# A two-layer Perceiver block on one core: normalization on VectorE, FP4 maxima in one reduce, biases added earlier, feed-forward split at 384 columns

## Chip, cores and metric

The kernel runs on one core of a Trainium2 chip. The metric is device time in microseconds. The kernel before took 1554.78 us, the median of three runs (1544.31 to 1555.05). Engines are named as in the profile: PE (matmul; PEld is its weight load), DVE (VectorE), ACT (ScalarE), POOL (GpSimd), SP (SyncE, which issues most transfers). An `Lnnn` is a line of the kernel before.

## What is computed

The input `x` has 16 sequences of 64 rows of 256 numbers, 1024 rows in all, and each sequence has a context of 1024 rows of 256. Each of two layers applies cross-attention to the context, self-attention and a feed-forward part, each on a layer-normalized copy of `x` and added back to it. In layer 0 self-attention goes across sequences, and the feed-forward part is a mixture of eight experts. The change concerns layer 1 (and the quantization of its weights). Cut to its core:

```
def _layernorm(x, eps=1e-05):
    m = mean(x); v = var(x)
    return (x - m) / sqrt(v + eps)

def fp4_quant_dequant(x):                 # blocks of 16 along the last dim
    scale = max(max(abs(xb)) / 6, 1e-12)
    xn = xb / scale
    idx = searchsorted(_MID, abs(xn))
    return _GRID[idx] * sign(xn) * scale

def _L1_xattn_ref(query, mem, ...):       # 16 heads of 16, bias and mask on keys
    return softmax(q @ k.T * scale + attn_bias + pad) @ v @ out_w.T + out_b

def _L1_attn_ref(x, w_qkv, w_proj, b_proj):   # rotary, 16 heads, 64 rows each
    return softmax(rope(q) @ rope(k).T * scale) @ v @ w_proj + b_proj

def _L1_ffn_ref(x, w_gate, w_up, w_down):     # 256 -> 704 -> 256
    h = silu(fp4(x) @ fp4(w_gate).T) * (fp4(x) @ fp4(w_up).T)
    return fp4(h) @ fp4(w_down).T

x = x + _L1_xattn_ref(_layernorm(x), ctx_1024, ...)
x = x + _L1_attn_ref(_layernorm(x), ...)
x = x + _L1_ffn_ref(_layernorm(x), ...)
```

## The kernel before

All data are 32-bit floats. The 1024 rows of `x` stay on chip as eight tiles `x[n]` of 128 rows (two sequences each). `consts` holds the identity for PE's transposes. PSUM has eight banks; in layer 1 seven rotate under the name `psw` (`bank()`), and one, `pso`, gathers attention outputs.

**Main loop of cross-attention.** Layer 1's cross-attention (`cross_attention`, L308 to L640) walks over 64 slots: 16 sequences x two groups of heads x two halves of the keys. Each slot issues on PE the scores of the slot after the next (L445), four groups of transposes of the exponentials `e` (L475), and the products of the slot before with `v` (L489). DVE reads the scores, adds the mask and finds the minimum (L456), ACT takes the exponential (L467), and both copy the transposes (L217, L219). Keys and values of nine sequences were made earlier and lie in DRAM; those of the other seven are projected inside the loop (L370, L385).

**Chains.** All work that follows on a pair of sequences is a Python generator, a *chain*, on row tile n. After every group of transposes the loop calls `advance()`, which runs each living chain on to its next `yield`, oldest first: four advances in a slot. A chain starts after the eighth slot of its pair, so a chain is 32 steps ahead of the next one while the loop lasts, and 28 at its end, where the last slot's work has no advances. PE's instructions are issued in exactly the order in which the program text produces them (`manual_schedule`); a PE instruction that waits holds up all behind it. The other engines' orders are made by a scheduler from dependences and its own estimates of duration. So the number of yields between two matmuls of a chain sets how much main-loop work lies between them on PE. When the loop is over, the two chains still living (n = 6 and n = 7) are advanced alternately until they end: the tail.

A chain's steps (the code between yields), counted from 1:

- `outputs`, steps 1 to 7: copy of `pso` (1), transposes L511 and division by the sums, L514 (3), transposes L527 and value bias, L531 (5), output projection `project_rows` L301 (7).
- `row_attention`: `layernorm_rows` (9), transposes L269 and copy L271 (12), queries and keys L1229, copy `ra` L1238, cosine part on POOL L1240 (14), rotation L1249 and sine part on DVE L1250 (16), sums L1258/L1259 and the masked queries `rqm` on POOL L1262 (17), values L1273 (18), scores L1286 and their minima and differences, L1297/L1298 (20, 21), exponential L1304 (22), transposes L1311 (24), products L1327 and sums L1338, reciprocal L1348 and L1349 (26, 27), projection L301 (29).
- `feed_forward`: `layernorm_rows` (31), FP4 of the 256 columns (34 to 37), transposes L269 (39), both halves of 352 hidden columns L1376, `Silu` L1379 and product L1380 (41), FP4 of the halves one after the other (42 to 49), all six transposes L1391 (51), down projection L1405, the last sum L1407 and the store L1408 (53).

**`layernorm_rows`** finds mean and variance on DVE (L244, L246), starts the reciprocal square root from the exponent bits (L248 to L253, DVE), makes three Newton steps of three instructions each on POOL, and applies the result on POOL (L260, 128x256). It then yields three times. It also serves the queries of cross-attention (`queries`, tile `xnq`, L269 and L405), which run ahead of the loop for n = 0 and in it for the others. `arrive` gathers the expert outputs of layer 0 for the next row tile by two indirect transfers on POOL (L1127) and adds them to `x[n]` on DVE (L1137) just before `xnq` is normalized.

**`fp4`** takes absolute values on ACT (L890), finds the blocks' maxima (L893), makes scale and reciprocal (L894 to L898), and scales (L899), rounds (L906 to L910) and scales back (L911) on DVE. `quantize_weights` uses it for the six weight blocks, beside layer 0's experts.

**`project_rows`** multiplies, adds the bias on DVE to `prow` (L303), and adds `prow` to `x[n]` on POOL (L304).

Of the kernel before, what the change touches and what calls it, by code (L numbers as in the profile page):

```python
# [19 lines left out]
P = 128  # L20
# [98 lines left out]
def kernel(ctx: ExitStack, tc: tile.TileContext, a: dict, out: bass.AP):  # L119
# [121 lines left out]
    def layernorm_rows(pool, n, name="xnr"):  # L241
# [55 lines left out]
    def project_rows(n, oT, w, bias):  # L297

        pm = bank()
        for c in range(KC):  # L300
            nc.tensor.matmul(pm[:, :D], oT[:, c, :], w[:, c, :], start=(c == 0), stop=(c == KC - 1))  # L301
        t = small.tile([P, D], F32, name="prow")
# [4 lines left out]
    def cross_attention(layer, wq, wkv, wo, bq, bk, bv, bo, mask, keep, bias, after, ready, arrive, idle):  # L307
        side = "right" if layer else "left"  # L308
        with ExitStack() as st:
# [84 lines left out]
            def queries(n):  # L394
# [3 lines left out]
                xn = yield from layernorm_rows(single, n, "xnq")  # L398
# [98 lines left out]
            def outputs(b):  # L497
# [38 lines left out]
                project_rows(n, oT, wo, rowbias(bo))  # L536
# [346 lines left out]
    def fp4(pool, dst, src, rows, n, tag, most=None):  # L883

        nb = n // BLK
        most = most or n
        shape = [rows, nb, BLK]
        t = pool.tile([P, most], F32, name=f"t{tag}")[:rows, :n]
        t3 = t.rearrange("p (g k) -> p g k", k=BLK)
        nc.scalar.activation(t, src, AF.Abs)  # L890
# [4 lines left out]
        rsc = pool.tile([P, most // BLK], F32, name=f"rsc{tag}")[:rows, :nb]  # L895
# [4 lines left out]
            t3, src.rearrange("p (g k) -> p g k", k=BLK), rsc.unsqueeze(2).to_broadcast(shape), ALU.mult  # L900
# [4 lines left out]
        m = pool.tile([P, most], F32, name=f"m{tag}")[:rows, :n]  # L905
# [257 lines left out]
    def quantize_weights(step, pool):  # L1163
        if step < 4:
# [9 lines left out]
            for _ in fp4(pool, q, raw, PG, n, "w"):  # L1174
# [12 lines left out]
        elif step < 6:  # L1187
# [4 lines left out]
            for _ in fp4(pool, q, raw, P, NI, "d"):  # L1192
# [15 lines left out]
    def last_layers(one):  # L1208
# [11 lines left out]
        def row_attention(n, two):  # L1220
            vz = vzs[n % 2]
            xn = yield from layernorm_rows(two, n)
# [134 lines left out]
            project_rows(n, oT, wproj, rowbias("L1_attn_b_proj"))  # L1357
# [3 lines left out]
        def feed_forward(n, two):  # L1361
            tok = slice(n * P, (n + 1) * P)
            xn = yield from layernorm_rows(two, n)
            yield from fp4(one, xn, xn, P, D, "h", NI)
# [5 lines left out]
            for g in range(2):  # L1370
                cols = slice(g * NH, (g + 1) * NH)
                pg = bank()[:, :NH]
                pu = bank()[:, :NH]
                for ps, w in ((pg, wgT), (pu, wuT)):
# [138 lines left out]
```

## Time and profile before

| | |
|---|---|
| median of three runs | 1554.78 us |
| profiled execution, its own time | 1553.52 us |
| its span, first to last instruction | 1551.8 us |
| mean granted PE clock | 0.942 |
| second layer's cross-attention begins (L269 on `xnq`) | at 871.6 us |
| last main-loop products (L489) end | at 1463.5 us |
| last store issued | at 1549.1 us |

Times within the run count from the first instruction. "Busy" is the time in which an engine works on an instruction. A row of the stage table gives a stretch, its length, and each engine's busy time in it (with the number of instructions), the granted PE clock as a share of full speed, the share of time that the transfers were busy, and GB/s. A row of the timeline gives start, duration, engine, line, operation, output from inputs, shapes, a count, and in brackets how long the engine was idle before it and what ended that. A row of the waits gives who waited for whom: time in total, number of times, the longest. The chain of waits that ended last:

```profile
PE 73%; DVE 12%; POOL 4%; ACT 4%; DMA 3%; issue 3%; ACTq 0%; POOLq 0%; DVEq 0%; SPq 0%
```

### The profile page before, as it was taken

To read this page: it belongs to the slowest core of one execution; us is meant where nothing else is said; L and a number is where in the kernel's file an instruction comes from. 1 tells how busy PE (TensorE), PEld (TensorE's weight loads), DVE (VectorE), ACT (ScalarE), POOL (GpSimd) and SP (SyncE) were. 2 spreads that over 40 slices of the span, in tenths; PEclk is the share of its full clock that TensorE was granted. 3 is DMA by queue.
4 is the path that set the end of the run, shared out by engine and by line. 5 is a ranking of instruction groups with operands and counts; after the bars stand their busy time and mean duration, and the time that the engine had idled before them with its cause. 6 is when DMAs were issued, how large, how long until landed. Compare 5 with 4: busy or idle time off the path is not lost.

```text
span 1551.8 us, 32601 instructions
## 1 busy us (share of the span) xinstructions
PE 1411.0 (91%) x13488; PEld 995.0 (64%) x13488; DVE 880.4 (57%) x2325; ACT 725.3 (47%) x1339; POOL 285.4 (18%) x502
## 2 busy tenths in 40 slices
PE   4999999999999998999999787888899999999754
PEld 2667766676667655768887555565657666666542
DVE  2556665656565533365721265675767675757543
ACT  2555555555555532223221475564656465646321
POOL 4101010000000031013300134241414141311111
PEclk8999999999999999999999798888889999999876
DMA  8111110101000021377774232322101111100000
GB/s 281 59 31 35 32 59 32 35 32 59 31 28 2 35 90 70 105 260 235 234 283 147 90 117 94 118 86 74 57 14 46 46 52 49 42 5 1 5 5 3
DMA packets 53073, 119.48 MB, mean 77 GB/s; under 512 B 4877, under 2 KB 24333, under 8 KB 50621
## 3 DMA queue, kind: packets, MB, share of 16 engines
q1 hardware_dynamic: 48876, 109.93, 21.0%
q0 software_dynamic: 1648, 4.72, 1.1%
q10 hardware_dynamic: 2400, 2.76, 0.5%
q8 instruction: 106, 1.74, 0.5%
q14 instruction: 43, 0.34, 0.1%
HBM read 94.32 MB, written 23.07 MB: 76 GB/s over the span
## 4 chain that ended last, share of the span: by engine, by line
PE 73%; DVE 12%; POOL 4%; ACT 4%; DMA 3%; issue 3%; ACTq 0%; POOLq 0%; DVEq 0%; SPq 0%
PE psw L475 11%; PE psw L385 10%; PE psw L370 9%; PE psw L445 8%; PE pso L489 7%; PE psw L659 4%; PE psw L1085 4%; PE psw L1105 4%; DVE e L456 3%; PE psw L646 3%; ACT e L467 3%; PE psw L1376 2%; PE psw L1405 2%; PE psw L301 2%; DMA kd<-astage 1%
## 5 line engine op out<-in xcount | busy, mean ns | idle before, releaser
L467 ACT ACTIVATE e<-e,mn 128x1024 f32<-128x1024 f32 x256 | 291.1, 1139 | 125.3 <-DVE mn L456 125.3
L475 PEld LDWEIGHTS psw<-consts,e 128*128 128x128 f32 x2048 | 242.6, 144 | 111.6 <-issue 64.3
L475 PE MATMUL psw<-consts,e 128*128 128x128 f32 x2048 | 286.8, 280 | 10.1 <-DVE mn L456 5.7
L456 DVE CUSTOM_DVE_ANT_0 e<-psw,negb,mn 128x512 f32<-128x512 f32 x256 | 177.9, 747 | 180.0 <-PE psw L445 180.0
L456 DVE CUSTOM_DVE_ANT_0 e<-psw,negb 128x512 f32<-128x512 f32 x256 | 162.9, 686 | 87.0 <-PE psw L445 86.8
L219 ACT COPY eT<-psw 128x512 f32<-128x512 f32 x320 | 174.1, 590 | 58.3 <-PE psw L475 57.9
L445 PE MATMUL psw<-kT,qm 32*128 32x512 f32 x1024 | 167.7, 690 | 3.4 <-ACT qm L415 1.8
L489 PE MATMUL pso<-eT,v 128*32 128x128 f32 x4096 | 146.0, 286 | 0.0
L370 PE MATMUL psw<-ctxT,w_L_xattn_Wkv 128*128 128x512 f32 x256 | 125.0, 612 | 11.9 <-DMA ctxT<-in_ctxT_dram 11.9
L217 DVE COPY eT<-psw 128x512 f32<-128x512 f32 x192 | 123.0, 678 | 9.3 <-PE psw L475 9.3
L489 PEld LDWEIGHTS pso<-eT,v 128*32 128x32 f32 x4096 | 109.4, 114 | 28.0 <-issue 25.9
L385 PE MATMUL psw<-w_L_xattn_Wkv,ctxT 128*128 128x256 f32 x512 | 123.6, 385 | 0.0
L385 PEld LDWEIGHTS psw<-w_L_xattn_Wkv,ctxT 128*128 128x128 f32 x512 | 93.0, 190 | 33.7 <-issue 11.9
L370 PEld LDWEIGHTS psw<-ctxT,w_L_xattn_Wkv 128*128 128x128 f32 x256 | 44.3, 192 | 68.4 <-issue 55.1
L219 ACT COPY v<-psw 128x512 f32<-128x512 f32 x46 | 27.0, 588 | 123.8 <-PE psw L385 123.8
L304 POOL TENSOR_TENSOR x<-x,prow 128x256 f32<-128x256 f32 x24 | 17.4, 727 | 315.1 <-DVE prow L303 315.1
L659 PE MATMUL psw<-w_L_xattn_Wkv_w,actx 128*128 128x256 f32 x288 | 73.4, 409 | 0.8 <-ACT astage L653 0.8
L445 PEld LDWEIGHTS psw<-kT,qm 32*128 32x128 f32 x1024 | 49.2, 197 | 37.8 <-issue 20.2
L337 POOL TENSOR_SCALAR negb<-m 128x1024 f32<-128x1024 uint8 x16 | 16.7, 1046 | 285.8 <-DVE mn L456 172.4
L380 ACT ACTIVATE kT<-psw,colb 128x512 f32<-128x512 f32 x48 | 32.8, 687 | 75.3 <-PE psw L370 75.3
L646 PE MATMUL psw<-actx,w_L_xattn_Wkv_w 128*128 128x512 f32 x144 | 66.2, 599 | 1.3 <-DVE x L632 1.3
L659 PEld LDWEIGHTS psw<-w_L_xattn_Wkv_w,actx 128*128 128x128 f32 x288 | 58.0, 206 | 13.6 <-issue 3.8
(248 smaller groups left out, 1974.0 us busy)
## 6 DMA issues: line engine op xcount, KB each, us to landing
ctxT<-in_ctxT_dram SPq DMA_DIRECT2D x23, 1024.0 KB, 5.0
w<-in_L_ffn_w_dram SPq DMA_DIRECT2D x16, 1024.0 KB, 6.9
actx<-in_ctxT_dram SPq DMA_DIRECT2D x9, 1024.0 KB, 6.8
kd<-astage SPq DMA_DIRECT2D x36, 256.0 KB, 3.7
vd<-astage SPq DMA_DIRECT2D x36, 256.0 KB, 2.4
kT<-kd SPq DMA_DIRECT2D x9, 1024.0 KB, 6.1
v<-vd SPq DMA_DIRECT2D x9, 1024.0 KB, 5.0
ab<-in_fside_BxS_dram SPq DMA_DIRECT2D x32, 256.0 KB, 3.4
```

The costliest lines, as they stand in the source:

```text
L217: nc.vector.tensor_copy(dst, src)
L219: nc.scalar.copy(dst, src)
L370: nc.tensor.matmul(pm, wkv[:, c, dt * P : (dt + 1) * P], ctxT[b][:, c, cols], start=(c == 0), stop=(c == KC - 1),)
L385: nc.tensor.matmul(pm[:, j * D : (j + 1) * D], ctxT[b][:, c, (k + j) * P : (k + j + 1) * P], wkv[:, c, D : 2 * D], start=(c == 0), stop=(c ...
L445: nc.tensor.matmul(sc[g], qm[b // 2][r : r + 32, dt, b % 2, :, :].rearrange("p j q -> p (j q)"), kT[b][r : r + 32, dt, cols], start=True, ...
L456: nc.vector.tensor_tensor_reduce(out=e[:, cols], in0=sc[g], in1=negb[b][:, cols], scale=1.0, scalar=3e38 if hf == 0 else mn[b][:, 0, pr : ...
L467: nc.scalar.activation(e, e, AF.Exp, scale=-1.0, bias=mn[b][:, 1, pr : pr + 1], accum_out=sums[b][:, pr : pr + 1])
L475: nc.tensor.transpose(pt[:, g * P : (g + 1) * P], es[b, dt, g][:, k * P : (k + 1) * P], ident)
L489: nc.tensor.matmul(po[b][32 * g : 32 * g + 32, dt, :], v[b][:, k, pr * 32 : (pr + 1) * 32], e[:, g, :], start=(k == 0), stop=(k == NK - 1),)
L646: nc.tensor.matmul(pm, w1kv[:, c, dt * P : (dt + 1) * P], actx[b][:, c, cols], start=(c == 0), stop=(c == KC - 1),)
L659: nc.tensor.matmul(pm[:, j * D : (j + 1) * D], actx[b][:, c, (k + j) * P : (k + j + 1) * P], w1kv[:, c, D : 2 * D], start=(c == 0), stop=( ...
L1085: nc.tensor.matmul(ph[:, j * CAP : (j + 1) * CAP], w1[:, c, (f + j) * P : (f + j + 1) * P], xeT[:, c, :], start=(c == 0), stop=(c == KC - 1),)
```

## The change

`layernorm_rows` gets a switch `vector`. With it, all Newton steps run on DVE, two instructions each (the factor -0.5 is multiplied into the variance once), the result is applied on DVE, and the function doesn't yield. It is set for `row_attention`, `feed_forward` and layer 1's first query tile; the other query tiles and layer 0 keep POOL. `row_attention` yields twice of its own instead of three times, `feed_forward` once.

In layer 1 `project_rows` no longer adds a bias: the product is added to `x[n]` by one DVE instruction. The biases are added to `x[n]` on POOL as soon as the normalized copy has been made: the output bias after `xnq`, the projection bias after `xnr`.

`fp4` has no ACT step and no yield for it: the reduce takes absolute values itself. Its tiles are made by a function of their own, so that two calls can work on parts of the same tiles.

The hidden columns are split 384 and 320 (three PE transposes each). For n up to 6 each half has its own step for matmuls and for transposes. For n = 7 (`alone`) everything from the first hidden matmul on is one step, in which the first half's transposes and its share of the down projection come ahead of the second half's quantization.

The chain's steps after the change, counted in the same way: `outputs` as before; `row_attention`: normalization 9, L269 11, L1229 13, L1249 15, L1262 16, L1273 17, L1286 19, L1304 21, L1311 23, L1327 25, L301 28; `feed_forward`: normalization 30, FP4 31 to 33, L269 35, L1376 37 and 38, FP4 39 to 44, L1391 46 and 47, L1405 49; for n = 7 all from L1376 on is step 37.

```diff
-    def layernorm_rows(pool, n, name="xnr"):
+    def layernorm_rows(pool, n, name="xnr", vector=False):
...
+        xn = pool.tile([P, D], F32, name=name)
+        if vector:
+            nc.vector.tensor_scalar(va, va, -0.5, None, ALU.mult)
+            for _ in range(3):
+                nc.vector.tensor_scalar(t, r, va, r, ALU.mult, ALU.mult)
+                nc.vector.scalar_tensor_tensor(r, t, 1.5, r, ALU.add, ALU.mult)
+            made[name] = nc.vector.tensor_scalar(xn, x[n], mv[:, 0:1], r, ALU.subtract, ALU.mult)
+            return xn
         for _ in range(3):
...
-        xn = pool.tile([P, D], F32, name=name)
         made[name] = nc.gpsimd.tensor_scalar(xn, x[n], mv[:, 0:1], r, ALU.subtract, ALU.mult)
...
-    def project_rows(n, oT, w, bias):
+    def project_rows(n, oT, w, bias=None):
...
+        if bias is None:
+            nc.vector.tensor_tensor(x[n], pm[:, :D], x[n], ALU.add)
+            return
...
-                xn = yield from layernorm_rows(single, n, "xnq")
+                xn = yield from layernorm_rows(single, n, "xnq", layer == 1 and n == 0)
+                if layer:
+                    nc.gpsimd.tensor_tensor(x[n], x[n], rowbias(bo), ALU.add)
                 xT = transposed_rows(single, xn, "xTq")
...
-                project_rows(n, oT, wo, rowbias(bo))
+                project_rows(n, oT, wo, None if layer else rowbias(bo))
...
-    def fp4(pool, dst, src, rows, n, tag, most=None):
+    def fp4_tiles(pool, tag, most):
+        return (
+            pool.tile([P, most], F32, name=f"t{tag}"),
+            pool.tile([P, most], F32, name=f"m{tag}"),
+            pool.tile([P, most // BLK], F32, name=f"scl{tag}"),
+            pool.tile([P, most // BLK], F32, name=f"rsc{tag}"),
+        )
+
+    def fp4(tiles, dst, src, rows, n, lo=0):
...
-        nc.scalar.activation(t, src, AF.Abs)
-        yield
-        scl = pool.tile([P, most // BLK], F32, name=f"scl{tag}")[:rows, :nb]
-        nc.vector.tensor_reduce(scl, t3, AX.X, ALU.max)
+        s3 = src.rearrange("p (g k) -> p g k", k=BLK)
+        nc.vector.tensor_reduce(scl, s3, AX.X, ALU.max, apply_absolute_value=True)
...
         def row_attention(n, two):
             vz = vzs[n % 2]
-            xn = yield from layernorm_rows(two, n)
+            xn = yield from layernorm_rows(two, n, "xnr", True)
+            nc.gpsimd.tensor_tensor(x[n], x[n], rowbias("L1_attn_b_proj"), ALU.add)
+            yield
+            yield
             xT = transposed_rows(two, xn)
...
-            project_rows(n, oT, wproj, rowbias("L1_attn_b_proj"))
+            project_rows(n, oT, wproj)
...
         def feed_forward(n, two):
...
-            xn = yield from layernorm_rows(two, n)
-            yield from fp4(one, xn, xn, P, D, "h", NI)
+            alone = n == NT - 1
+            xn = yield from layernorm_rows(two, n, "xnr", True)
+            yield
+            yield from fp4(fp4_tiles(one, "h", NI), xn, xn, P, D)
             yield
             xT = transposed_rows(two, xn)
             yield
             yield
...
-            for g in range(2):
-                cols = slice(g * NH, (g + 1) * NH)
-                pg = bank()[:, :NH]
-                pu = bank()[:, :NH]
...
+            def hidden(cols):
+                w = cols.stop - cols.start
+                pg = bank()[:, :w]
+                pu = bank()[:, :w]
+                for ps, wt in ((pg, wgT), (pu, wuT)):
...
                 nc.scalar.activation(h[:, cols], pg, AF.Silu)
                 nc.vector.tensor_tensor(h[:, cols], pu, h[:, cols], ALU.mult)
...
+            def turn_hidden(g):
...
+            def down(g):
+                for j in range(g, g + 3):
+                    w = min(P, NI - j * P)
+                    nc.tensor.matmul(py, hT[:w, j, :], wdT[:w, j, :], start=(j == 0), stop=(j == NCH - 1))
...
+            halves = [slice(0, 3 * P), slice(3 * P, NI)]
+            if alone:
+
+                hidden(halves[0])
+                tiles = fp4_tiles(one, "h", NI)
+                first = fp4(tiles, h[:, halves[0]], h[:, halves[0]], P, 3 * P)
+                next(first)
+                hidden(halves[1])
+                for _ in first:
+                    pass
+                turn_hidden(0)
+                py = bank()[:, :D]
+                down(0)
+                for _ in fp4(tiles, h[:, halves[1]], h[:, halves[1]], P, NI - 3 * P, 3 * P):
+                    pass
+                turn_hidden(3)
+                down(3)
+            else:
+                for cols in halves:
+                    hidden(cols)
+                    yield
+                for cols in halves:
+                    yield from fp4(fp4_tiles(one, "h", NI), h[:, cols], h[:, cols], P, cols.stop - cols.start)
+                yield
+                turn_hidden(0)
+                yield
+                turn_hidden(3)
+                yield
+                yield
+                py = bank()[:, :D]
+                down(0)
+                down(3)
             y = small.tile([P, D], F32, name="prow")
             nc.vector.tensor_tensor(y, py, x[n], ALU.add)
```

More of the change, by code (lines that the diff above doesn't have):

```diff
@@ L899, in fp4 @@
         nc.vector.tensor_tensor(
-            t3, src.rearrange("p (g k) -> p g k", k=BLK), rsc.unsqueeze(2).to_broadcast(shape), ALU.mult
+            t3, s3, rsc.unsqueeze(2).to_broadcast(shape), ALU.mult
         )
         yield
-        m = pool.tile([P, most], F32, name=f"m{tag}")[:rows, :n]
         nc.vector.tensor_scalar(m.bitcast(I32), t.bitcast(I32), 0x7F800000, None, ALU.bitwise_and)
@@ L1173, in quantize_weights @@
             q = pool.tile([P, n], F32, name="qres")[:PG]
[L1174 removed]
+            for _ in fp4(fp4_tiles(pool, "w", n), q, raw, PG, n):
                 pass
@@ L1380, in feed_forward @@
                 nc.vector.tensor_tensor(h[:, cols], pu, h[:, cols], ALU.mult)
-            yield
-            for g in range(2):
-                cols = slice(g * NH, (g + 1) * NH)
-                yield from fp4(one, h[:, cols], h[:, cols], P, NH, "h", NI)
-            yield
-            hT = one.tile([P, NCH, P], F32, name="hT")
-            for g in range(0, NCH, 3):
+            def turn_hidden(g):
                 pt = bank()
```

19 lines of the change are left out of this document (7 added, 12 removed).

## The prediction

> **What bounds the kernel now.** I read the page's busy time first, then busy time by stage, then PE's waits over the last 112 us, then the timeline of the end. Times within the run are from the span's start; "6" and "7" are the chains of the last two row tiles, n = 6 and 7.
>
> ```profile
> PE 1411.0 (91%) x13488; PEld 995.0 (64%) x13488; DVE 880.4 (57%) x2325; ACT 725.3 (47%) x1339; POOL 285.4 (18%) x502
> ```
>
> PE bounds the span as a whole, but the change touches only the second layer, so the stages count (columns: stretch, length, busy time of PE, PEld, DVE, ACT, POOL, granted clock):
>
> ```profile
> 960.00:1040.00 80.00, 71.19 (x750) 50.12 (x747) 56.99 (x162) 46.33 (x89) 26.25 (x46) 0.87 0.25 83
> ...
> 1360.00:1440.00 80.00, 77.68 (x762) 54.50 (x755) 54.82 (x151) 44.45 (x84) 15.25 (x30) 1.00 0.01 3
> 1440.00:1470.00 30.00, 21.23 (x338) 16.96 (x336) 13.27 (x38) 12.43 (x26) 4.10 (x11) 0.93 0.02 6
> 1470.00:1552.00 82.00, 40.36 (x240) 26.61 (x240) 34.04 (x92) 14.26 (x27) 10.39 (x25) 0.67 0.01 4
> ```
>
> Up to 1440 PE is the bound: 77.68 of 80 us. From 1470 no engine is: PE has half, at a granted clock of 0.67. That is the stretch in which the main loop has ended and only chains 6 and 7 run. PE's waits from 1440 on name the links:
>
> ```profile
> PE psw L269 <- DVE xnr L911: 11.1, 1, 11.1
> PE psw L1391 <- DVE h L911: 10.7, 3, 4.4
> PE psw L301 <- DVE oT L531: 4.4, 1, 4.4
> PE psw L269 <- POOL xnr L260: 3.8, 1, 3.8
> ```
>
> and the timeline shows them in place:
>
> ```profile
> 1479.72 0.69 PE L269 MATMUL psw<-consts,xnr 128*128 128x128 f32 x2 [3.82 <-POOL xnr L260]
> ...
> 1494.10 1.99 PE L1286 MATMUL psw<-rkT,rqm 32*128 32x64 f32 x32 [3.11 <-POOL rqm L1262]
> ...
> 1502.97 1.97 PE L1311 MATMUL psw<-consts,ra 128*128 128x128 f32 x8 [2.98 <-ACT ra L1304]
> ...
> 1504.73 4.02 PE L1405 MATMUL psw<-wdT,hT 128*128 128x256 f32 x12
> ...
> 1508.68 0.80 PE L1327 MATMUL psw<-turned,vz 64*32 64x64 f32 x60
> ...
> 1513.90 0.72 POOL L304 TENSOR_TENSOR x<-x,prow 128x256 f32<-128x256 f32 x1 [19.86 <-DVE prow L303]
> ...
> 1518.96 1.22 POOL L260 TENSOR_SCALAR xnr<-x,mvr,rsd 128x256 f32<-128x256 f32 x1
> 1520.21 0.42 ACT L890 ACTIVATE th<-xnr 128x256 f32<-128x256 f32 x1 [14.65 <-POOL xnr L260]
> ...
> 1543.44 5.21 PE L1405 MATMUL psw<-wdT,hT 128*128 128x256 f32 x12
> ```
>
> One dependent line leads from L269 (chain 7) to the store: every microsecond cut from it in the tail shortens the run. L1405 at 1504.73 belongs to chain 6 and stands in chain 7's way only because PE's order is written by hand.
>
> **Part 1, chain 7's second normalization (on the path).** Old: rsd ready 1515.86, xnr ready 1520.18, 4.32 us on POOL. New, on DVE: seven 128x1 steps at the pitch of L251 to L253 (0.19 us) = 1.33, plus a 128x256 tensor_scalar, 0.41 in the first layer's L234 group, plus a gap = 1.8 us. The step with two pointer scalars isn't shown on DVE; bounds are L251's 0.15 and POOL's L256, 0.34 busy, so 0 to +0.5 over the three; I take 0, as the nearest rows are DVE's. Gain 2.5. The bias added earlier: L303's start 1513.40 to bnst 1514.66 is 1.26, of which one DVE add (0.45 with its gap) stays: gain 0.8. FP4's maxima straight from xnr: L890 1520.21 to L893 1520.66: gain 0.45. An absolute reduce isn't in the trace; the same reduce without it is (L893, 0.42), bounds 0.42 and 0.42+0.42 if it read twice; I take 0.42. Sum 3.75.
>
> **Part 2, chain 7's feed-forward alone (on the path).** Old: L1376 at 1525.62, L1405's end 1548.65: 23.0. New, from L1376's start: 384 columns for gate and up take 5.1 x 384/352 = 5.5 (the first eight old matmuls: 1525.62 to 1530.7); DVE then does two products (0.55, 0.48) and both quantizations without a gap. One 352-column quantization after its ACT step is 1538.02 to 1542.29, 4.27; 384 and 320 columns make 4.45 and 4.1. Sum 5.5 + 1.03 + 8.55 + gaps 0.1 = 15.2 against the old 16.7. The second half's matmuls and the first half's transposes and L1405s lie beside DVE. Left after DVE: transposes and copy 1.15, then six of twelve L1405 records, 5.21/2 = 2.6. End 19.0: gain 4.0. If the cover were gone (the early half of L1405 run last), 2.6 comes back.
>
> **Part 3, order on PE in the tail (on the path).** Chains are advanced in turn, chain 6 28 steps ahead (seven slots of four). Counting the yields: before, chain 6's L269, L1376, L1391, L1405 are its steps 39, 41, 51, 53 and come just before chain 7's steps 12 (L269), 14 (L1229), 24 (L1311), 26 (L1327), as in the timeline. After, they are steps 35, 37 and 38, 46 and 47, 49: L269 comes ahead of chain 7's out-projection L301 (step 7), both L1376 groups ahead of 7's L269 (step 11), both transposes ahead of L1286 (step 19), L1405 ahead of L1311 (step 23). Worked on:
> chain 6's tiles are ready 3.75 us sooner, but 7's L301 now queues on PE behind 6's L269, so it ends near 1471.8 (old 1472.1). L1376, 16 records, 5.7 us (some at the low clock), to 1477.5; in that time DVE makes 7's normalization (3 us from 1471.85). L269, copy, then L1229 at 1478.4 (old 1486.33). Now L1286 waits for 6's second transposes, which wait for DVE: from 1475.4, products 1.0, quantizations 8.55, chain 7's L1250 and L1258/59 1.5, and 1.0 lost beside POOL (below) = 12.05, to 1487.5; transposes 1.1; L1286 at 1488.6 (old 1494.10). Its 2.0, eight uncut L1297/L1298 at 0.43 = 3.5, the table load 1.28 and exponential 1.06: L1311 at 1496.5 (old 1502.97); 1.3 sooner if the load comes before the wait, as at 1480.84. L1405 lies in that wait, so L1311 to L1327 shrinks from 5.7 to the copies' 2.65: L1327 at 1499.1, or 1497.8; gain 9.6 to 10.9, taken as 10.2.
>
> Tail: 3.75 + 4.0 + 10.2 = 18.
>
> **Part 4, the second layer's main loop.** PE waited for xnq on POOL four times there, 12.0 us. At 1025.16 (2.26) and 1101.36 (2.54) POOL was busy with the other tile's normalization (xnr ended 1020.17, xnq began 1020.15): that queue is gone, gain 4.8. At 954.59 (3.59, and 3.36 for xnr before it) xnq's statistics now wait behind 1.8 us more DVE work: 0. At 904.76 no xnr is in the way: 0. Against it stands DVE: 14 normalizations x 1.8 = 25 us more. In most of the loop PE is full and DVE idle 25 of 80 us, which hides them; but in 1013 to 1026, where the chain normalizes, DVE has hardly a gap. Bounds 0 and 25; I take 2, nearer to zero because the PE-bound rows are most of the loop. ACT loses 24 L890 of 0.42 to 0.5, all but the tail's beside work: 0 (ACT idles 34 of 80; without that, 10 more). The first query tile's move to DVE is worth 0: its POOL step ended at 857.1 (855.87 + 1.23), and PE was busy with projections and L269 came only at 871.6. The six weight quantizations lose their ACT step in a stage where PE is busy 113.5 of 120: 0. The bias adds leave POOL's count at 16 x 0.72, but move them beside DVE work, xnq's behind its tile, and ahead of the next gather (L1127), which has 60 us to spare. Net gain 3.
>
> On contention: L908 took 1.53 us at 1489.15 while POOL ran L1240, 0.53 otherwise, and L907 0.72 against 0.29 while POOL ran L304. I count the first once. At 0.43 for each of 16 bias adds it would be 7 us of DVE time, again mostly under PE.
>
> The Trainium skill, "GPSIMD Engine Reference", section 8 (Key points), says that GpSimd shares its SBUF interfaces with VectorE and collides with DVE instructions that read two SBUF inputs or use two ports. The two rows agree in kind but show a part of the time lost, not all. If each bias add shut DVE out for its whole 0.72 and nothing hid it, that rule would take 11.5 off the gain, an estimate, and leave 9.5 of 21.
>
> **Sum.** 18 + 3 = 21. The profiled execution took 1553.52 (span 1551.8 and 1.7 around it): 1532.5. The median of the three runs is 1.3 higher: 1534. One of the three was 1544.31, 10 below, so a spread of 10 lies on any single figure.
>
> **Rivals.**
> (a) The main loop gains more: all 15.4 us of PE's waits for L260's results go, and with them the low clock after them (0.83 to 0.87 at 960 to 1120, 1.00 later). For: the loss of clock follows the stalls. Against: 904.76 and 954.59 have other causes. Price 8 to 12 more: 1523 to 1526.
> (b) DVE sets the middle of the tail: transposes ahead of L1286 make chain 7 wait for all of chain 6's DVE work, and if DVE's order also puts 6 ahead of 7's L1250 and normalization, part 3 shrinks to 2 to 5. For: L301 waited 4.4 on oT behind chain 6's L893 just so. Then 10 to 13 in all: 1542 to 1545.
> (c) Slower: DVE becomes the bound of the main loop. Its 25 us of normalizations and 7 of collisions reach PE; above 21/32, two thirds exposed, the change loses. Fully exposed: 32 - 18 = +14, 1569. For: no gap at 1013 to 1026. Against: 25 of 80 us idle on the whole.
> (d) The two-pointer step and the absolute reduce at their upper bounds: 0.5 + 0.42 x 3 on the path, 2 us. It stays inside the main range.
>
> **Numbers.** No change is anything within 1%, about what a measurement of this kernel can tell (1539.2 to 1570.3). Forecast 0.58, own range 1527 to 1541, a seventh of it above 1539; (a) 0.12; (b) 0.20; (c) 0.10, of which 0.06 lies over 1570 (full exposure is 1569, and the spread lies on it). Faster 0.50 + 0.12 = 0.62; same 0.08 + 0.20 + 0.04 = 0.32; slower 0.06. The range 1517 to 1549 takes in (a) and (b) with the spread and leaves (c) out.
>
> **What would show it.** Right: after the main loop PE's order L1376, L269, L1229 and L1405 ahead of L1311; the last L269 near 8.5 us after the last L301 (1512.23 to 1524.49, 12.3, before); last L1376 to last L1405's end near 19; no POOL row of 128x1 but xnq's. Wrong: the last slots' transposes before 1440 come later than before (c), or L1286 in the tail waits on h for over 5 us (b).

## The result and the profile after

The change makes the kernel slower by a little: 1555.88 us (median of 15 runs) against 1544.31 (15 runs of the kernel before, taken with them), a ratio of 1.0068 with a 95% interval of 1.0050 to 1.0086. The forecast was 1534. The profiled execution of the changed kernel took 1557.56 us, its span 1555.5.

Lines are those of the changed kernel from here on: normalization L244 to L267, its transposes L276 (L269 before), projections of rows L308 (L301) with the addition L310, FP4 L912 to L928, row attention L1249 to L1347 (L1229 to L1327), hidden matmuls L1400 (L1376), their transposes L1410 (L1391), down projection L1425 (L1405).

The busy time of the page, over the whole run (engine, busy us, share, instructions):

```profile
PE 1408.4 (91%) x13488; PEld 998.5 (64%) x13488; DVE 896.2 (58%) x2461; ACT 714.1 (46%) x1309; POOL 225.2 (14%) x332
```

PE did the same work in a longer span, DVE 16 us more (880.4 before), POOL 60 less. Busy time by stage, in the same columns as before, says where the time went:

```profile
960.00:1040.00 80.00, 63.44 (x680) 45.77 (x682) 51.84 (x162) 41.55 (x78) 18.93 (x26) 0.83 0.23 77
...
1360.00:1440.00 80.00, 74.11 (x686) 51.56 (x685) 49.50 (x143) 42.82 (x81) 9.84 (x17) 0.96 0.05 16
1440.00:1470.00 30.00, 28.26 (x275) 21.51 (x273) 20.00 (x61) 15.90 (x31) 2.93 (x4) 1.00 0.02 6
1470.00:1556.00 86.00, 53.19 (x524) 37.04 (x523) 48.76 (x146) 20.88 (x40) 3.43 (x4) 0.79 0.01 4
```

From 960 to 1040 PE was busy 63.4 of 80 us (71.2 before), from 1360 to 1440 74.1 (77.7). DVE and ACT were busy less there, too: no engine became the bound. PE lost time in the main loop and gained some after it.

I cut the span at two marks that every kernel here has: the first L276 on `xnq` of layer 1, at about 872, and the last transposes of an attention output (L523; L511 before). Between them lies the main loop, behind them the tail.

| | span | main loop | tail |
|---|---|---|---|
| before | 1551.8 | 592.4 | 87.8 |
| after | 1555.5 | 613.5 | 70.0 |

The tail is shorter by 17.8, the main loop longer by 21. The profiled execution of before lay 9.2 us above the median of its 15 runs, and a kernel with its steps and engines in the loop took 584.3 there (`e_tail_only` below); against that the main loop lost 29. The two make +11.4, and the medians differ by 11.6.

PE's waits from 870 to 1455 (who waited for whom: us in total, times, longest):

```profile
PE psw L276 <- POOL xnq L267: 38.9, 7, 8.1
PE psw L276 <- DVE xnr L261: 12.0, 3, 5.5
PE psw L1400 <- ACT xTr L278: 5.7, 3, 2.9
```

The same view of before, with nothing on DVE `xnr`:

```profile
PE psw L269 <- POOL xnq L260: 12.0, 4, 3.6
PE psw L301 <- DVE oT L1349: 10.2, 6, 2.9
...
PE psw L269 <- POOL xnr L260: 3.4, 1, 3.4
```

The waits for normalized tiles rose from 15.4 to 50.9 us; those for `oT`, 10.2, are gone. A third row is new, the hidden matmuls' wait for their own input `xTr`. One slot of the kernel before shows the old order on PE, with the hidden matmuls (L1376, the first of four rows) between L301 and the transposes of `xnr`:

```profile
1012.07 1.03 PE L301 MATMUL psw<-w_L_xattn_out_w,oT 128*128 128x256 f32 x4
1013.80 1.35 PE L1376 MATMUL psw<-wgT,xTr 128*128 128x352 f32 x4
...
1022.49 0.41 PE L269 MATMUL psw<-consts,xnr 128*128 128x128 f32 x2 [0.25 <-POOL rsd L258]
1025.16 0.44 PE L269 MATMUL psw<-consts,xnq 128*128 128x128 f32 x2 [2.26 <-POOL xnq L260]
```

One slot of the changed kernel shows what happens (timeline; start, duration, engine, line, and in brackets the wait before it):

```profile
1093.38 1.24 PE L1400 MATMUL psw<-wgT,xTr 128*128 128x320 f32 x4
...
1095.97 1.03 PE L308 MATMUL psw<-w_L_xattn_out_w,oT 128*128 128x256 f32 x4
...
1098.53 0.48 DVE L1404 TENSOR_TENSOR h<-psw,h 128x320 f32<-128x320 f32 x1
...
1099.45 0.41 DVE L310 TENSOR_TENSOR x<-psw,x 128x256 f32<-128x256 f32 x1
...
1106.11 0.41 DVE L261 TENSOR_SCALAR xnr<-x,mvr,rsd 128x256 f32<-128x256 f32 x1
...
1106.67 0.66 PE L276 MATMUL psw<-consts,xnr 128*128 128x128 f32 x2 [5.46 <-DVE xnr L261]
...
1107.86 0.35 ACT L278 COPY xTr<-psw 128x256 f32<-128x256 f32 x1
...
1114.27 0.69 PE L276 MATMUL psw<-consts,xnq 128*128 128x128 f32 x2 [6.08 <-POOL xnq L267]
...
1115.61 2.93 PE L1249 MATMUL psw<-xTr,w_L_attn_w_qkv 128*128 128x128 f32 x16
```

L1400 belongs to the older chain's feed-forward, L308 to the younger chain's cross-attention. The hidden matmuls come first on PE. So their products and FP4 are on DVE when L308 ends at 1097.0, L310 begins only at 1099.45, and from there to the end of `xnr` DVE alternates between the younger tile's normalization, the older tile's FP4 (2.1 us, from start to next start) and, as it is late, the main loop's next four minima (L468, 2.7 us): 7.1 us. PE has only the main loop's own work left to put between L308 and the transposes of `xnr`, then `xnq`, and waits 5.46 and 6.08. The last two rows show what a wait costs those behind it: L1249 needs only `xTr`, which ACT had copied by 1108.21, but stands behind the transposes of `xnq` and starts at 1115.61. The Trainium skill, "PSUM — Partial Sum Buffer", section "Engine vs sequencer instructions", says that matmuls start and complete in program order; these rows agree, 7.4 us after L1249's input was there.

### The profile page after: what moved, and what is told of

Read it like the earlier page. It is cut to its first block, busy times and chain, and to the rows that moved or that the text cites. A ratio compares the mean times of both kernels' runs of the same rounds, so it can differ in the third digit from the quotient of the medians.

```text
span 1555.5 us, 32501 instructions
## 1 busy us (share of the span) xinstructions
PE 1408.4 (91%) x13488; PEld 998.5 (64%) x13488; DVE 896.2 (58%) x2461; ACT 714.1 (46%) x1309; POOL 225.2 (14%) x332
## 4 chain that ended last, share of the span: by engine, by line
PE 75%; DVE 13%; ACT 5%; DMA 3%; issue 3%; POOL 2%; ACTq 0%; SPq 0%; POOLq 0%; DVEq 0%
PE psw L487 11%; PE psw L380 10%; PE psw L395 9%; PE psw L457 8%; PE pso L501 7%; DVE e L468 4%; PE psw L1102 4%; PE psw L1122 4%; PE psw L671 3%; ACT e L479 3%; PE psw L658 3%; PE psw L1400 2%; PE psw L1425 2%; PE psw L1249 1%; PE psw L417 1%
## 5 line engine op out<-in xcount | busy, mean ns | idle before, releaser
L468 DVE CUSTOM_DVE_ANT_0 e<-psw,negb,mn 128x512 f32<-128x512 f32 x256 | 178.6, 747 | 173.0 <-PE psw L457 173.0
L468 DVE CUSTOM_DVE_ANT_0 e<-psw,negb 128x512 f32<-128x512 f32 x256 | 163.2, 686 | 119.5 <-PE psw L457 118.8
L457 PE MATMUL psw<-kT,qm 32*128 32x512 f32 x1024 | 163.3, 665 | 1.8 <-ACT qm L427 1.8
L501 PE MATMUL pso<-eT,v 128*32 128x128 f32 x4096 | 140.6, 279 | 0.0
L501 PEld LDWEIGHTS pso<-eT,v 128*32 128x32 f32 x4096 | 106.0, 111 | 23.0 <-issue 21.1
L395 PEld LDWEIGHTS psw<-w_L_xattn_Wkv,ctxT 128*128 128x128 f32 x512 | 93.0, 190 | 33.7 <-issue 11.6
L457 PEld LDWEIGHTS psw<-kT,qm 32*128 32x128 f32 x1024 | 50.3, 190 | 34.2 <-issue 18.3
L665 ACT ACTIVATE astage<-psw,colb 128x512 f32<-128x512 f32 x36 | 24.6, 687 | 78.7 <-PE psw L658 45.7
```

Of the source, the lines that this page charges most:

```text
L395: nc.tensor.matmul(pm[:, j * D : (j + 1) * D], ctxT[b][:, c, (k + j) * P : (k + j + 1) * P], wkv[:, c, D : 2 * D], start=(c == 0), stop=(c ...
L457: nc.tensor.matmul(sc[g], qm[b // 2][r : r + 32, dt, b % 2, :, :].rearrange("p j q -> p (j q)"), kT[b][r : r + 32, dt, cols], start=True, ...
L468: nc.vector.tensor_tensor_reduce(out=e[:, cols], in0=sc[g], in1=negb[b][:, cols], scale=1.0, scalar=3e38 if hf == 0 else mn[b][:, 0, pr : ...
L501: nc.tensor.matmul(po[b][32 * g : 32 * g + 32, dt, :], v[b][:, k, pr * 32 : (pr + 1) * 32], e[:, g, :], start=(k == 0), stop=(k == NK - 1),)
```

## The experiments

The letters in the expectations: S says that the main loop lost by the steps (the hidden matmuls come four steps earlier, 37 and 38 against 41; the row attention's transposes one, 11 against 12); Q that it lost by the query tiles left on POOL behind a longer queue on DVE. The plain rival, D, is the prediction's (c), that DVE has too much work. All edits are to the changed kernel. Ratios are to the kernel before on the same chip (medians 1546.02, 1548.80 and 1551.72 in the three groups of four).

**`a_steps_before`: normalization stays on DVE, all of the chain's steps as before.**

```diff
             nc.gpsimd.tensor_tensor(x[n], x[n], rowbias("L1_attn_b_proj"), ALU.add)
             yield
             yield
+            yield
...
             xn = yield from layernorm_rows(two, n, "xnr", True)
             yield
+            yield
+            yield
+            yield
...
                 for cols in halves:
                     hidden(cols)
-                    yield
+                yield
                 for cols in halves:
+                    yield
                     yield from fp4(...)
                 yield
                 turn_hidden(0)
-                yield
                 turn_hidden(3)
```

> The changed kernel with yields put back, so that every matmul of the chains of n = 0 to 6 stands at the step it had before (L269 at 12 and 39, L1376 at 41, L1391 at 51); normalization stays on DVE, FP4 without its ACT step, biases early, n = 7's feed-forward alone. Main loop means here from layer 1's first L269 on xnq to the last transposes of the attention output: 592.4 us before (871.6 to 1464.0), 613.5 after (872.1 to 1485.6); tail is the rest of the span: 87.8 and 70.0. Theory S (the steps: fewer yields moved the hidden columns' FP4 into the slot in which the next chain and the next query tile are normalized, and PE comes to their transposes too early): main loop back to 589 to 597, tail 80 since only chain 7's own parts of 3.75 and 4.0 us are left; in all 8 us faster than before. Theory D (DVE's load: the normalizations moved there hold up the scores and xnq's statistics wherever they stand): main loop stays above 605, in all 3 to 12 us slower than before.

Measured: ratio 0.9882 [0.9831, 0.9933], main loop 580.9, tail 75.2. All DVE work of the change is in it (910.5 us busy, more than in the changed kernel), and the loss is gone: (c) falls. The tail I had expected near 80.

**`b_ln_on_pool`: the steps of the change, main-loop normalizations back on POOL.**

```diff
-            xn = yield from layernorm_rows(two, n, "xnr", True)
+            xn = yield from layernorm_rows(two, n, "xnr", n == NT - 1, True)
...
-            xn = yield from layernorm_rows(two, n, "xnr", True)
+            xn = yield from layernorm_rows(two, n, "xnr", n >= NT - 2, True)
```

(The last argument makes the POOL form return without its own yields.)

> The changed kernel, with all its steps where the change put them, but the normalizations of the main loop (row attention of n = 0 to 6, feed-forward of n = 0 to 5) made on POOL again. Theory S: the main loop stays long, 610 to 625, and PE's wait for xnr is longer than the 12.0 us after the change, as POOL needs 4.3 us where DVE needs 1.8. Theory D: main loop back to 592 to 598, tail 70, in all 13 to 18 us faster than before.

Measured: 0.9971 [0.9946, 0.9996], main loop 597.8, tail 69.6; PE waited 23.3 us for `xnq` and 17.8 for `xnr`.

**`e_tail_only`: steps and POOL in the main loop as before, the tail of the change.** In the feed-forward for n below 6, and in the row attention for n below 7, it has both a's yields and b's POOL; the rest is the change.

> Chains of n = 0 to 5 and the row attention of n = 6 at the steps and with the normalization engine of before (POOL), the feed-forward of n = 6 and all of n = 7 as after the change; FP4 without its ACT step and early biases everywhere. If the tail's gain (17.8 us in the two profiles) and the main loop's loss (21.1) are separate, as both S and D say: main loop 589 to 596, tail 69 to 72, ratio to before 0.986 to 0.991. If the tail's gain depended on the changed main loop, tail over 78.

Measured: 0.9871 [0.9820, 0.9922], main loop 584.3, tail 68.2. So the tail's part of the change, with its smaller edits elsewhere, brings 1.3%. The four make a table of the main loop:

| main loop, us | normalization on POOL | on DVE |
|---|---|---|
| steps of before | 584.3 (e) | 580.9 (a) |
| steps of after | 597.8 (b) | 613.5 (after) |

With the old steps DVE is 3.4 better. The new steps cost 13.5 with POOL and 32.6 with DVE: the loss belongs to the steps, and it is larger by 19 with DVE. These are single profiles: the profiled runs of the experiments lie between 4.4 us below (`m_two_later`) and 3.2 above (`l_later_not_in_tail`) the median of their kernel's runs, so the 3.4 is within that scatter and the other two are not.

PE does the same work in each of these loops (5436 or 5437 matmuls), so a loop's length is PE's busy time on it and its idle time. The loops of a and of the changed kernel, in the columns of the stage table:

```profile
872.70:1453.62 580.92, 526.52 (x5437) 368.54 (x5437) 415.41 (x1208) 334.90 (x630) 118.40 (x159) 0.94 0.17 55
872.09:1485.55 613.46, 537.32 (x5436) 378.96 (x5437) 401.79 (x1209) 336.25 (x630) 112.66 (x159) 0.92 0.15 52
```

PE idles 54.4 us in a and 76.1 after the change, and by the same view 52.2 in e and 67.2 in b. So the new steps cost 15.0 of idle time with POOL and 21.7 with DVE, and DVE adds 6.7 of waiting to the loss, not 19. The rest is PE's busy time on the same matmuls (532.1 in e, 526.5 in a, 530.7 in b, 537.3 after), whose differences no run here explains.

**`c_queries_on_dve`: all query tiles on DVE too, with three yields for those that went.**

```diff
-                xn = yield from layernorm_rows(single, n, "xnq", layer == 1 and n == 0)
+                xn = yield from layernorm_rows(single, n, "xnq", layer == 1)
...
+                if layer and n:
+                    yield
+                    yield
+                    yield
```

> The changed kernel with layer 1's query tiles n = 1 to 7 normalized on DVE too, yields as they are (PE's order is the changed kernel's). Theory Q (the long part of the wait for xnq, 38.9 us in seven times, is POOL's 4.3 us behind a late DVE): 2.5 us less in each of seven, main loop near 596 to 600. Theory S: DVE is behind in that slot in any case, so at most half of that, main loop 603 to 612. Theory D: seven more normalizations of 1.8 on DVE, main loop 613 to 625.

Measured: 0.9998 [0.9969, 1.0027], main loop 600.4, tail 69.1. It lands at Q's edge. Q has a part, 13 us; but PE still waited 26.7 us for `xnq`, seven times, and 11.6 for `xnr`, now all on DVE.

Then which step? S1: the place of the hidden matmuls against the younger chain's L308 (step 7) and L276 (step 11). With 32 steps between chains, steps 37 and 38 fall on the younger chain's 5 and 6, ahead of L308; step 41 falls on 9, between the two. S2: the one step less in the row attention.

**`f_hidden_later`: four yields ahead of the hidden matmuls**, which makes them steps 41 and 42.

```diff
+            if not alone:
+                for _ in range(4):
+                    yield
             h = one.tile([P, NI], F32, name="h")
```

> The changed kernel with four yields more ahead of the first hidden matmul for n = 0 to 6: L1376 at steps 41 and 42, FP4 of the hidden columns from 43, its transposes at 50 and 51; everything ahead of that (L269 at 11 and 35, normalization on DVE) as the change has it. So far the main loop took 613.5 (after), 597.8 (steps of after, POOL), 580.9 (steps of before, DVE), 584.3 (steps of before, POOL). Theory S1 (of the steps it is the hidden columns' part, whose products and FP4 now stand ahead of the next chain's normalization on DVE): main loop 580 to 592, the wait for xnr under 3 and for xnq under 22. Theory S2 (it is the yields between normalization and its L269): main loop stays above 603. The tail is 74 to 78, as chain 6 is later there too.

Measured: 0.9801 [0.9752, 0.9850], main loop 571.7, tail 74.5. Nearly all of the loss goes, and more. PE's waits in its main loop (870 to 1440; the wait for `xnr` from L261 has fallen to 1.1, the one for `xTr` is gone):

```profile
PE psw L276 <- POOL xnq L267: 19.3, 4, 8.1
```

The slot from the timeline of `f_hidden_later` (PE alone; L1403 are the hidden matmuls):

```profile
1077.01 1.03 PE L308 MATMUL psw<-w_L_xattn_out_w,oT 128*128 128x256 f32 x4
1078.75 1.46 PE L1403 MATMUL psw<-wgT,xTr 128*128 128x384 f32 x4
1080.04 1.45 PE L1403 MATMUL psw<-wuT,xTr 128*128 128x384 f32 x4
...
1084.00 1.24 PE L1403 MATMUL psw<-wgT,xTr 128*128 128x320 f32 x4
1085.08 1.24 PE L1403 MATMUL psw<-wuT,xTr 128*128 128x320 f32 x4
1086.70 0.44 PE L276 MATMUL psw<-consts,xnr 128*128 128x128 f32 x2
...
1091.98 0.69 PE L276 MATMUL psw<-consts,xnq 128*128 128x128 f32 x2 [3.77 <-POOL xnq L267]
```

L308 comes first, DVE normalizes at once, and PE does 5.4 us of hidden matmuls meanwhile. L276 then has no wait for `xnr`. DVE's rows from L310 on are only the normalization, ending 1082.40, with the hidden product behind it (timeline of `f_hidden_later`, DVE):

```profile
1081.99 0.41 DVE L261 TENSOR_SCALAR xnr<-x,mvr,rsd 128x256 f32<-128x256 f32 x1
1082.32 1.34 DVE L1154 SCALAR_TENSOR_TENSOR x<-g,rt_w,x 128x256 f32<-128x256 f32 x2
1083.58 0.54 DVE L1407 TENSOR_TENSOR h<-psw,h 128x384 f32<-128x384 f32 x1
```

**`g_row_yield`: the row attention's third yield back, alone.**

```diff
             nc.gpsimd.tensor_tensor(x[n], x[n], rowbias("L1_attn_b_proj"), ALU.add)
             yield
             yield
+            yield
```

> The changed kernel with one yield more between the row attention's normalization and its transposes (L269 at step 12, as before; all later steps one later, L1376 at 38 and 39). Theory S2: the wait for xnr (12.0) goes and main loop falls to 585 to 598. Theory S1: L1376 is still two to three steps early, and PE waits for xnq instead: main loop 603 to 613.

Measured: 1.0043 [1.0012, 1.0074], main loop 611.2, tail 70.2. S2 falls as the cause. PE's waits (870 to 1455) are even longer than in the changed kernel:

```profile
PE psw L276 <- POOL xnq L267: 47.9, 7, 8.6
PE psw L308 <- DVE oT L1370: 10.2, 6, 2.9
```

The 10.2 us on `oT` that before had are back, and the wait for `xnq` is 9.0 longer; the one for `xnr` is 3.3 shorter (8.7), and there is none for `xTr`. In all PE idles 86.5 us in g's loop against 76.1, so by its waits the shorter row attention is a gain of the change. The length of the loop doesn't show it (611.2 against 613.5), as PE was busy 524.8 in g and 537.3 in the changed kernel. f against a does: f has 0.4 us of waits on `oT` and a 12.0, PE is busy alike (526.9, 526.5), and f's loop is 9.2 shorter.

**`k_fp4_later`: hidden matmuls as in the change, four yields between them and their FP4.**

```diff
                 for cols in halves:
                     hidden(cols)
                     yield
+                for _ in range(4):
+                    yield
                 for cols in halves:
```

> The changed kernel with four yields more between the hidden matmuls (steps 37 and 38, as the change has them) and the FP4 of their result (from step 43, transposes at 50 and 51). It parts the matmuls and products from the 8.5 us of FP4 on DVE. Theory S1 in the form that FP4's place in the program sets DVE's order: main loop 582 to 595. If DVE takes FP4 as soon as its input is there, whatever the yields: above 605.

Measured: 1.0105 [1.0054, 1.0155], main loop 618.4, tail 69.5, waits for `xnq` and `xnr` 39.0 and 12.0, as in the changed kernel. In its timeline FP4's L912 (1093.97) to L928 (1100.12) still runs ahead of L310 (1101.52): DVE's order isn't the written one but the scheduler's, and FP4 is still done as soon as its input is there. Here yields held PE's matmuls, not DVE's work; to move FP4 its matmuls had to move. k also puts the later transposes and the down projection where f has them, so it isn't these that make f's gain.

**`i_steps_and_tail`: a's main loop and the tail of the change**, the edit of a for the chains below the last two.

> Normalization on DVE throughout; chains of n = 0 to 5 and the row attention of n = 6 at the steps of before, the feed-forward of n = 6 and all of n = 7 as after the change. Main loop as with the steps of before and DVE (580.9), 578 to 584; tail as after the change, 68 to 71; in all 21 to 27 us less than before, ratio 0.983 to 0.987, the fastest so far.

Measured: 0.9824 [0.9786, 0.9861], main loop 580.7, tail 68.5, the ratio just under what I had put down. Both gains add up.

**`l_later_not_in_tail`: f, with n = 6 left as in the change.**

```diff
+            if n < NT - 2:
+                for _ in range(4):
+                    yield
             h = one.tile([P, NI], F32, name="h")
```

> As the kernel with four yields more ahead of the hidden columns, but with these yields for n = 0 to 5 only, so that the tail is the changed kernel's. Main loop as with the four yields (571.7), 570 to 574; tail 68.5 to 70.5 instead of 74.5: 4 to 6 us less than that kernel, ratio to before 0.975 to 0.980.

Measured: 0.9747 [0.9716, 0.9777], 1511.89 us, main loop 569.9, tail 68.9. It is the fastest of the series together with o, 2.5% below the kernel before and 3.2% below the change (0.9747/1.0068, from two chips).

**`m_two_later` and `n_eight_later`: f with 2 and with 8 yields in place of 4.** By S1 two put the halves on steps 7 and 8 of the younger chain, eight on 13 and 14, behind L276.

> The changed kernel with two yields more ahead of the first hidden matmul (L1376 at steps 39 and 40, against the next chain's steps 7 and 8: just before its out-projection and ahead of its normalization at 9). Theory S1 (what counts is whether the hidden products and FP4 come ahead of the next chain's normalization on DVE): main loop still long, 598 to 613. If it's only that PE comes to the transposes earlier by so many steps, half the loss goes: 588 to 597.

> The changed kernel with eight yields more ahead of the first hidden matmul (L1376 at 45 and 46, against the next chain's 13 and 14). Theory S1: normalization and xnq are free of FP4 as with four, main loop 566 to 578; FP4 then meets L1250, L1258 and the minima L1297 of the next chain, which PE reaches at its steps 15 to 23, and 2 to 4 us may be lost there.

Measured: 0.9884 [0.9846, 0.9923], main loop 586.6, tail 67.2; and 0.9893 [0.9852, 0.9934], main loop 586.6, tail 71.4. Both figures missed what I had put down for S1: two did better, and lies next to the other reading's 588 to 597, by which half the loss goes; eight did worse. The slot of `n_eight_later` (timeline, PE) explains the second:

```profile
1084.40 1.03 PE L308 MATMUL psw<-w_L_xattn_out_w,oT 128*128 128x256 f32 x4
1090.55 0.41 PE L276 MATMUL psw<-consts,xnr 128*128 128x128 f32 x2 [1.15 <-DVE xnr L261]
1099.49 0.69 PE L276 MATMUL psw<-consts,xnq 128*128 128x128 f32 x2 [8.09 <-POOL xnq L267]
1100.82 2.77 PE L1403 MATMUL psw<-wgT,xTr 128*128 128x384 f32 x4
```

DVE is free of FP4, and from L308 to the transposes of `xnq` it takes 15.1 us, as in f (15.0), against 18.3 in the changed kernel. But the hidden matmuls now come after that stretch, and PE waits 8.09 of it. I had seen one effect of the early matmuls, FP4 in the way on DVE; they have a second, that PE lacks the work which covers the normalization. Across this slot of all five kernels:

| kernel | L1400 between L308 and L276 | from L308 to `xnq`'s L276 | waits for `xnq`, times, loop | main loop | PE idle in it |
|---|---|---|---|---|---|
| after | none, all ahead | 18.3 | 38.9, 7 | 613.5 | 76.1 |
| m, two later | second half | 18.4 | 41.5, 7 | 586.6 | 66.6 |
| n, eight later | none, all behind | 15.1 | 35.1, 7 | 586.6 | 60.0 |
| f, four later | both halves | 15.0 | 19.3, 4 | 571.7 | 44.8 |
| a, steps of before | both halves | 14.0 | 17.6, 4 | 580.9 | 54.4 |

f against n is in the main the cover: 14.9 us of the loop, 15.2 of idle time. It isn't the cover alone, since n's FP4 also falls on a later stretch of the younger chain. After against n, neither of which has cover, is 26.9 of the loop but 16.1 of idle time. Of that 5.7 is the wait for `xTr`, which n doesn't have, and the waits for `xnr` and `xnq` are 12.4 shorter in n: the collision on DVE. The other 10.8 is again PE's busy time on the same matmuls. m is as long as n by chance: PE idles 6.6 more in it and is busy 6.6 less. By idle time m, with half the matmuls as cover, gets back 9.5 of the 31.3 that f gets back; its waits for `xnr` fell from 12.0 to 4.1, its stretch to `xnq` stayed as long as the change's.

**`o_later_and_queries`: l and c together.**

> As the kernel with four yields more for n = 0 to 5, and the query tiles n = 1 to 7 normalized on DVE as well. PE still waits 19.3 us for xnq in four places there (3.6, 8.1, 3.8, 3.8), and DVE needs 2.5 us less than POOL in each: main loop 3 to 10 us less than with the four yields alone, 562 to 569, if DVE has room; 572 to 580 if the seven normalizations (12.6 us of DVE) hold up the scores.

Measured: 0.9760 [0.9730, 0.9791], main loop 566.7, tail 69.6; PE's wait for `xnq` 13.8. The main loop is 3.2 shorter than l's in the profile, but o's profiled run lay 4.0 below its median and l's 3.2 above; the whole is not to be told from l.

## Why the prediction was wrong

**The base.** The forecast of 1534 starts from a median of 1554.78, which is 10.5 above the median of the 15 runs (1544.31). Counted as a difference, 21 less were forecast and 11.6 more came.

**The tail held.** 18 were forecast, 17.8 came (87.8 to 70.0), so close only because one part was larger than forecast and another smaller. In its pieces: to the start of row attention's last products (L1327, now L1347) from the end of the main loop 44.7 before, 33.3 after, 11.4 for part 3's 10.2. The timeline of the changed kernel has PE's order as worked out:

```profile
1491.20 0.69 PE L276 MATMUL psw<-consts,xnr 128*128 128x128 f32 x2 [2.87 <-DVE xnr L928]
1491.69 1.91 PE L308 MATMUL psw<-w_L_xattn_out_w,oT 128*128 128x256 f32 x4
1493.39 2.77 PE L1400 MATMUL psw<-wgT,xTr 128*128 128x384 f32 x4
...
1509.76 0.55 PE L1410 MATMUL psw<-consts,h 128*128 128x128 f32 x3 [4.12 <-DVE h L928]
1510.23 1.98 PE L1306 MATMUL psw<-rkT,rqm 32*128 32x64 f32 x32
1512.14 5.39 PE L1425 MATMUL psw<-wdT,hT 128*128 128x256 f32 x12
...
1522.62 1.10 PE L308 MATMUL psw<-w_L_attn_w_proj,oT 128*128 128x256 f32 x4 [2.28 <-DVE oT L1369]
1531.25 0.66 PE L276 MATMUL psw<-consts,xnr 128*128 128x128 f32 x2 [7.52 <-DVE xnr L928]
...
1550.12 2.25 PE L1425 MATMUL psw<-wdT,hT 128*128 128x256 f32 x6 [0.46 <-ACT hT L219]
```

L1306 starts 24.7 after the main loop's end (1485.55); part 3 put it at 1488.6 - 1464.0 = 24.6. The wait on h ahead of it is 4.12, under the 5 that would have spoken for rival (b), and (b) did not occur. Part 1: last L308 to last L276 8.63 (12.26 before), gain 3.63 for 3.75. The step with two pointer scalars (L259) takes 0.27 where 0.15 was taken, so that the normalization lasts 2.0 from `rsd` on (1525.42 to 1527.45) and not 1.8; of (d) some of this part occurred, and not the other, as the reduce with absolute values takes 0.42. Part 2: L1400 at 1532.37 to the end of L1425 at 1552.37 is 20.0, not 19.0: gain 3.0 for 4.0. There the order on DVE was off, as its rows show:

```profile
1543.18 0.55 DVE L927 TENSOR_TENSOR th<-th,mh 128x384 f32<-128x384 f32 x1
1543.65 0.32 DVE L923 TENSOR_SCALAR mh<-th 128x320 int32<-128x320 int32 x1
1543.89 0.55 DVE L928 TENSOR_TENSOR h<-th,sclh 128x384 f32<-128x384 f32 x1
...
1544.59 0.87 PE L1410 MATMUL psw<-consts,h 128*128 128x128 f32 x3 [4.69 <-DVE h L928]
...
1545.76 0.49 DVE L928 TENSOR_TENSOR h<-th,sclh 128x320 f32<-128x320 f32 x1
...
1546.08 2.93 PE L1425 MATMUL psw<-wdT,hT 128*128 128x256 f32 x6 [0.62 <-ACT hT L219]
...
1548.81 0.85 PE L1410 MATMUL psw<-consts,h 128*128 128x128 f32 x3
```

The two quantizations run woven into each other, not one after the other as I took them. All of DVE's work ends 13.9 after L1400 (1546.25), earlier than the 15.2 worked out, but the first half ends late, at 1544.44, and its share of L1425 then stands on PE ahead of the second transposes until 1549.01: it is not covered, the case that part 2 priced at 2.6.

**The main loop failed, and with it the sign.** Part 4 forecast a net gain of 3 and has no term for the moved steps: the step that failed is this, that the new order on PE was put at nothing in the main loop. What part 4 priced, the move from POOL to DVE at unchanged steps, is a against e, and that gave 3.4. The agreement is luck: PE's idle time grew by 2.2 (52.2 to 54.4), and its busy time on the same matmuls fell by 5.6. Part 4 took the change's steps only into the tail. Part 3 had counted them itself (L269 and L1376 "are steps 35, 37 and 38") and worked out PE's new order from them; the same count in the main loop, where chains are 32 steps apart, puts L1376 on the younger chain's steps 5 and 6 in place of 9, ahead of L301 in place of behind it. That order is worked out from the text alone. Left out, it cost 13.5 with POOL and 32.6 with DVE, 15.0 and 21.7 of it PE's idle time.

**Smaller points of part 4.** The 4.8 us for POOL's queue at 1025 and 1101 did not come even with the old steps: a waits 17.6 for `xnq`, e 13.0. In a's slot of this kind (L276 on `xnq` at 1099.12, wait 2.70) POOL had itself waited 2.79 for DVE's `rsd`: its queue was gone, and DVE's came in its place, what the prediction granted for 954.59 alone. DVE's load was put at 14 normalizations and 25 us, 2 of it exposed; 13 fall in the loop, a's loop has 21.9 us more of DVE's work than e's (415.4 against 393.5), and PE idles 2.2 more there. The removed waits on `oT` (10.2) weren't foreseen. Slips in the rivals change nothing in the forecast: 12 more than 1534 is 1522, not (a)'s 1523, and rows of 80 us have 0.87 and 0.85 where it has 0.83 to 0.87, and 0.91 from 1120 to 1200; (b)'s 10 to 13 leaves out part 4's 3; (c) counts that 3 in its threshold of 21 and leaves it out of 32 - 18.

**Rival (c)** had the sign, and by coincidence 29 of its 32 us came, but not its mechanism: DVE is busy 51.8 of 80 where PE loses most, less than before (57.0), and a carries the same load without loss. Its trigger, a share of DVE's load exposed, would have said nothing about the remedy; the steps did. Its sign in the profile, the main loop's last transposes coming later, is there.

**The clock**, which rival (a) looked at from the gaining side, went the other way: 0.83 at 960 to 1040 (0.87 before), 0.89 in f. The Trainium skill, "TensorE: Matmul & The Clock Gate", Part 1, has the clock halved after an idle window of about 3.4 us; waits of 5 to 8 us with a lower mean clock around them agree in kind. No run here sets the clock apart from the waits, and the loops don't order by it: at a mean clock of 0.92 PE was busy 537.3 in the changed kernel's loop and 524.8 in g's.

## What to carry to other kernels

Where PE's order is written out and several chains are woven into a loop, taking steps out of a chain moves every later matmul of it against the neighbouring chain, all through the loop and not only at its end: lay the two chains' steps side by side, modulo their distance, at each stage that the change touches. Ask two things at each place, what covers the younger chain's latency on PE and what the older chain's matmuls release onto DVE. An edit that is right at the end can be kept to the last chains, as l does with one condition.

## What the hardware showed beside this

The normalization's 128x1 instructions on DVE took 0.14 to 0.27 us in the mean, so its chain of small steps (1524.90 to 1527.04 in the changed kernel) is as long as five 128x256 instructions of 0.42; woven with another tile's FP4 and the main loop's minima the whole, from the addition to `xnr`, stretched from 3.7 us (a, 1086.61 to 1090.29) to 7.1. POOL's addition of the projection bias (128x256, seven times in the loop) took 0.90 us in the median and 0.73 at its fastest; that DVE's work beside it is what stretched it wasn't isolated.
